# Turning x and x1 by transfers of squares and VectorE's transposes: two attention layers on one core

## The chip, the core and the metric

The kernel runs on one core of a Trainium2 chip. The metric is the device time of one execution in microseconds (us): lower is better. The engines named below are TensorE (PE: matmuls, and PEld: its weight loads), VectorE (DVE), ScalarE (ACT), GpSimd (POOL) and SyncE (SP, which here only issues transfers). All data are 32-bit floats. SBUF is the on-chip memory of 128 partitions; PSUM holds what TensorE writes, in banks of 512 floats a partition.

## What is computed

The input is 8 images of 32 x 32 positions with 256 channels, so 1024 rows of 256 for each image. Two layers follow each other:

```python
# layer 0, four heads
q, k, v = split(x @ W_qkv, per head)
a = softmax(q @ k.T / 16)                   # 1024 x 1024 for each head
x1 = concat(a @ v) @ W_out + b_out + x
# layer 1, one head
f, g, h = x1 @ Wf + bf, x1 @ Wg + bg, x1 @ Wh + bh     # f, g: 32 wide; h: 256 wide
y = gamma * (softmax(g @ f.T) @ h) + x1
```

Both layers need their input in two forms. As rows (positions on partitions) x is the value operand of layer 0 and x1 the residual of layer 1. As columns (channels on partitions: x^T and x1^T) they are operands of the score and projection matmuls. The change is about how the second form is made from the first.

## The kernel before

`W_q W_k^T` and `W_v W_out` are folded into one matrix for each head at the start, so that a head needs one projection of x^T. Large matmuls of layer 0 are done by a seven-product scheme on 2 x 2 blocks (`seven`, tasks one, two, three), whose operand sums VectorE makes: `key_sums` from x^T, `value_sums` from x, `sums` from the exponentials, `qsums` from the queries. VectorE also adds the products together when it empties PSUM banks (L252). Within one group of seven products TensorE goes on adding into banks y and z after VectorE has read them, so TensorE's second and third task wait for VectorE's reads of the first and second.

The work is a list of steps. A step is one block of 512 queries of one head of layer 0, or of layer 1. Images follow each other, and the layer-1 unit of image b-1 is put after head 1 of image b (after head 3 for the last image). In step i TensorE computes the scores of step i, and beside them the products of the steps before (`one` is step i-1, `two` is step i-2).

The order in which TensorE, VectorE and ScalarE execute is written out by hand. In the loop over steps (L805) each task gets a place, a number between about 0 and 10, by `put(tasks, places)`; at the end of a step the tasks are sorted by place and emitted. Every engine executes its own instructions in that order, and an instruction that waits holds up all behind it on its engine. Scores stand at 0, 2, 4, 6, 8, 10, the output projection (`project`, L586 and L597) at 3 and 7, the two parts of the products at 5 and 9.

`transpose_rows` (L331 to L344) makes the columns. Each of its four tasks takes a bank of the `psm` pool (2 banks), has TensorE transpose four 128 x 128 blocks of rows into it (L339), and has ScalarE copy the bank into x^T or x1^T (L342). It runs at the start for image 0; in the first block of head 3 for x of the next image, at places 1.5 to 4.5, with `key_sums` at 5.4 to 7.4; in the first block of the head ahead of the layer-1 unit for x1 of the image before, at places 2.5 to 8.5; and at the end for x1 of the last image.

The sums of exponentials go another way: GpSimd adds them over the partitions, and SyncE sends the row through DRAM and back as columns (`line`, L546, then `st`, L549), with `invert` (L555) reading them one step later. These transfers, the loads of x (L120) and the stores of the result (L675, L677) share SyncE's queue.

Buffers that matter: pool `q` has 2 buffers of 128 x 2 x 1024, which hold the queries of a head, or f and g of layer 1; `xT` has 2; `rows` 4; `ps` is 6 PSUM banks for scores and products, `psm` 2.

Of the kernel before, what the change touches and what calls it, by code (L numbers as in the profile page):

```python
# [16 lines left out]
P = 128  # L17
# [3 lines left out]
def kernel(  # L21
# [51 lines left out]
    nc = tc.nc  # L73
    B, H, W, C = x.shape
    N = H * W
    HEADS = w_qkv.shape[1] // (3 * C)
    CK = w_f.shape[1]
    CC = C // P
    NT = N // P
    NB = 512  # L80
    NBLK = N // NB
    HT = NB // P
    HB = NB // 2
    HN = N // 2
# [24 lines left out]
    def tile_of(tag, shape, name):  # L109
        return pools[tag].tile(shape, F32, tag=tag, name=name)  # L110


    rows, rows1 = {}, {}
# [78 lines left out]
    def sum_a(sums, a11, a12, a21, a22):  # L192
        tt = nc.vector.tensor_tensor
        s1, s2, s3, s4 = sums
        return [
            partial(tt, s1, a21, a22, ALU.add),
            partial(tt, s2, s1, a11, ALU.subtract),
            partial(tt, s3, a11, a21, ALU.subtract),
            partial(tt, s4, a12, s2, ALU.subtract),
        ]  # L200
# [128 lines left out]
    xT_of, x1T_of, xblocks, vblocks = {}, {}, {}, {}  # L329

    def transpose_rows(b, src, dst, layer):  # L331


        def task(k, c):
            if b not in dst:
                dst[b] = tile_of("xT", [P, CC, N], f"x{layer}T_{b}")
            pt = tile_of("psm", [P, NB], f"px{layer}_{b}_{k}_{c}")
            for t in range(HT):
                nc.tensor.transpose(  # L339
                    pt[:, ts(t, P)], src[b][:, k * HT + t, ts(c, P)], ident  # L340
                )
            nc.scalar.copy(dst[b][:, c, ts(k, NB)], pt)  # L342

        return [partial(task, k, c) for k in range(NBLK) for c in range(CC)]  # L344

    def key_sums(b):

        made = {}

        def piece(i):  # L350
            if i == 0:
                xT = xT_of[b]
                t = tile_of("v", [P, 4, HN], f"xs_{b}")
                sums = [t[:, k, :] for k in range(4)]
                blocks = [xT[:, c, ts(k, HN)] for k in range(2) for c in range(CC)]
                made["l"] = sum_a(sums, *blocks)
                xblocks[b] = a_operands(blocks, sums)
            made["l"][i]()

        return [partial(piece, i) for i in range(4)]  # L360
# [75 lines left out]
    class Layer0:  # L436
        def __init__(self, b, h):
            self.b, self.h, self.name = b, h, f"{b}_{h}"
            self.p, self.y, self.r = {}, {}, {}
            self.products_of, self.pblocks = {}, {}  # L440
            self.first = (b * HEADS + h) * NBLK * HT

        def queries(self):

            b, h = self.b, self.h

            def quarter(d, k):
                if d == 0 and k == 0:
                    self.q = tile_of("q", [P, CC, N], f"q_{self.name}")
                return self.q[:, d, ts(k, HN)].unsqueeze(1)  # L450

            def after():
                t = tile_of("qs", [P, 3, NBLK, HB], f"qs_{self.name}")
                q = self.q.rearrange("p c (k e i) -> p c e k i", k=NBLK, e=2)
                blocks = [q[:, c, e] for c in range(CC) for e in range(2)]
                sums = [blocks[1]] + [t[:, k] for k in range(3)]
                self.pieces = sum_b(sums, *blocks)
                self.blocks = b_operands(blocks, sums)

            def piece(k):  # L460
                self.pieces[k]()  # L461

            return seven(
                f"q_{self.name}", NB, 1,
                lambda number: [(0, wblocks[h][number], xblocks[b][number])],
                {
                    "11": lambda: quarter(0, 0), "12": lambda: quarter(1, 0),
                    "21": lambda: quarter(0, 1), "22": lambda: quarter(1, 1),
                },
                WIDE, nc.scalar.copy, after,  # L470
            ), [partial(piece, k) for k in range(4)]
# [132 lines left out]
    class Layer1:  # L604
        scale = 1.0

        def __init__(self, b):
            self.b, self.name = b, f"{b}_l1"
            self.s = {}

        def store_fg(self, d, k, pm):

# [5 lines left out]
        def queries(self):  # L618
            b = self.b

            def start():
                t = tile_of("q", [P, 2, N], f"fg_{b}")
                self.f, self.g = t[:, 0, :], t[:, 1, :]

            return [start] + project_T(
                f"fg_{b}", lambda: wfg_sb, P, lambda: x1T_of[b], self.store_fg
            )
# [122 lines left out]
    def weave(*lists):  # L750
# [12 lines left out]
        s=2, rows=4, xT=2, v=2, q=2, qs=2, xt=1, ss=1, s2=1, s3=1, m0=1, rs=1, rb=1,  # L763
# [32 lines left out]
    def is_l0(s):  # L796
        return s is not None and isinstance(s[0], Layer0)

    def step(k):
        return steps[k] if 0 <= k < len(steps) else None  # L800
# [4 lines left out]
    for i, (a, blk) in enumerate(steps):  # L805
        l0 = isinstance(a, Layer0)
        one, two, nxt = step(i - 1), step(i - 2), step(i + 1)
        places = []

        def put(tasks, *at):  # L810
            assert len(tasks) == len(at)
            places.extend(zip(at, range(len(places), len(places) + len(at)), tasks))

        if l0:
            put(a.scores(blk), 0, 2, 4, 6, 8, 10)
        else:
            tasks, pieces = a.scores(blk)
            put(tasks, *((0.5, 2.4) if blk == 0 else (0.5, 2)))
            put(pieces, *((1.6, 3.9, 6.2, 6.5, 7.4, 8.4, 8.6) if blk == 0 else
                          (0.9, 2.7, 4.2, 5, 6.2, 6.8, 7.5)))  # L820
        if is_l0(two):
            u, k = two
            put(u.products_of[k][2:], 1 if l0 else 0)
            put([partial(u.invert, k)], 2.9 if l0 or blk == 1 else 1.9)
            put(u.project(k), *((3, 7) if l0 else (2, 6) if blk == 0 else (3, 7)))
        if is_l0(one):
            u, k = one
            sums, keys = u.sums(k)
            u.products_of[k] = u.products(k)
            put(sums[:2] + sums[3:], *((2.2, 3.2, 4.2) if l0 else (0.8, 2.2, 4.5)))  # L830
            put(sums[2:3], 5.2 if l0 else 5.5)
            put(keys, *((6.2, 8.2) if l0 else (7.6, 9.6)))
            put(u.products_of[k][:2], *((5, 9) if l0 else (4, 7)))
        elif one is not None:
            put(one[0].products(one[1]), *((3, 5, 7, 9) if l0 else (1, 4, 6, 8)))
        if i == 0:
            fold = fold_weights(1) + fold_weights(2) + fold_weights(3)
            put(fold, -2, -1, *[0.9 + 0.6 * n for n in range(len(fold) - 2)])
        if i == 1:
            put([partial(nc.vector.tensor_scalar, bh_sb, bh_sb, gamma_sb, None, ALU.mult)], 8.5)  # L840

        if is_l0(nxt) and blk == NBLK - 1:
            queries, qsums = nxt[0].queries()
            put(queries, *((2.5, 4.5, 6.5) if not l0 else
                            (1.5, 2.5, 4.5) if is_l0(two) else (0.5, 2.5, 5.5)))
            put(qsums, *((6.7, 6.9, 7.3, 7.6) if not l0 else
                          (5.4, 6.4, 7.2, 7.4) if is_l0(two) else (6.4, 7.2, 7.3, 7.4)))

        if l0 and a.h == 0 and blk == 0:
            put(residual(a.b), 5.3, 6.3, 7.3, 7.4)  # L850
        if l0 and a.h == 0 and blk == 1:
            put(value_sums(a.b), 1.4, 2.4, 3.4, 4.4)
        if l0 and a.h == 2 and blk == 0 and a.b + 1 < B:
            load_x(a.b + 1)
        if l0 and a.h == HEADS - 1 and blk == 0 and a.b + 1 < B:
            put(transpose_rows(a.b + 1, rows, xT_of, 0), 1.5, 2.5, 3.5, 4.5)
            put(key_sums(a.b + 1), 5.4, 6.4, 7.2, 7.4)

        if l0 and a.b > 0 and a.h == behind(a.b) - 1:
            if blk == 0:  # L860
                put(transpose_rows(a.b - 1, rows1, x1T_of, 1), 2.5, 4.5, 6.5, 8.5)
            else:
                put(nxt[0].queries(), 1.4, 1.5, 3.5)
        if not l0 and blk == 0:
            put(a.values(), 0.9, 1, 3, 5, 8)
        if nxt is None:
            put(transpose_rows(B - 1, rows1, x1T_of, 1), 8.1, 8.2, 8.3, 8.4)
            put(final.queries(), 9, 9.1, 9.3)
        for _, _, t in sorted(places, key=lambda x: x[:2]):
            t()  # L870
# [82 lines left out]
    with tc.If(bad > 0), ExitStack() as general:  # L953
        open_pools(general, "g", dict(
            s=2, rows=2, xT=2, v=2, q=2, m0=1, y=1, rs=1, rb=2, r=8, ps=6, psm=2,
# [3 lines left out]
        for b in range(B):  # L959
# [3 lines left out]
            for h in range(HEADS):  # L963
                a = General0(b, h)
# [4 lines left out]
            a = Layer1(b)  # L969
# [37 lines left out]
```

## Time and profile before

The time is 2381.99 us, the median of 3 runs (2380.85 to 2382.96). The profiled execution spans 2379.7 us.

| engine | busy us | share of the span |
|---|---|---|
| TensorE, matmuls | 2361.3 | 99% |
| TensorE, weight loads | 1948.2 | 82% |
| VectorE | 1585.2 | 67% |
| ScalarE | 621.9 | 26% |
| GpSimd | 236.4 | 10% |
| transfers, main queue | | 3.2% of 16 engines |

Busy time counts how long an engine had an instruction in it; matmuls overlap each other, so a busy TensorE can hold short pauses, and the duration of one matmul is longer than the distance from its start to the next. A row of a group gives line, engine, operation, out<-in, shapes and count; after the bar the busy time and the mean of one in ns; after the second bar how long the engine stood idle just before these instructions, and what ended most of that idleness. A row of the timeline gives start (us from the span's beginning), duration, engine, line, operation, and the number of instructions merged into it.

### The profile page before, as it was taken

The numbers are of one execution on the slowest core, as the hardware profiler recorded it, in microseconds if no ns is written. First come the engines' busy times: TensorE is split into PE (matmuls) and PEld (weight loads), VectorE is DVE, ScalarE is ACT, GpSimd is POOL, SyncE is SP. The second block draws the span as 40 slices with busy tenths as digits, with TensorE's granted clock in tenths as the row PEclk, the third lists the DMA queues.
The fourth block names the chain that finished last, engine by engine and source line by source line (L and its number), as shares of the span: only waits on it lengthen the run. The fifth ranks groups of instructions, "written<-read, shape, count | busy, mean of one in ns | idle before, by whom it ended". The sixth has DMA issues, their size and how long they took to land.

```text
span 2379.7 us, 25958 instructions
## 1 busy us (share of the span) xinstructions
PE 2361.3 (99%) x10608; PEld 1948.2 (82%) x10608; DVE 1585.2 (67%) x2477; ACT 621.9 (26%) x1001; POOL 236.4 (10%) x93
## 2 busy tenths in 40 slices
PE   8999999999999999999999999999999999999999
PEld 6888888788887888788887888878888788888877
DVE  5667767567675666766667567676676756766665
ACT  2222223222232222322123222232222322122232
POOL 0111100011110111101111011110011101001110
PEclk9999999999999999999999999999999999999999
DMA  3000000000000000000000000000000000000000
GB/s 118 1 1 1 1 18 1 18 1 4 16 1 18 1 19 1 1 18 1 18 1 1 18 1 18 1 1 18 1 18 1 1 19 1 1 1 1 1 10 29
DMA packets 43535, 23.63 MB, mean 10 GB/s; under 512 B 36048, under 2 KB 38096, under 8 KB 43408
## 3 DMA queue, kind: packets, MB, share of 16 engines
q1 hardware_dynamic: 43408, 21.90, 3.2%
q8 instruction: 85, 1.39, 0.2%
q14 instruction: 42, 0.34, 0.1%
HBM read 13.37 MB, written 8.52 MB: 9 GB/s over the span
## 4 chain that ended last, share of the span: by engine, by line
PE 96%; DVE 3%; DMA 0%; issue 0%; ACT 0%; SPq 0%; DVEq 0%; ACTq 0%
PE psy L235 14%; PE psy_y L235 14%; PE pa_l L730 9%; PE po L586 9%; PE psx L235 9%; PE psz L235 9%; PE psx_y L235 9%; PE psz_y L235 9%; PE psy_q L235 3%; PE psx_q L235 2%; PE psz_q L235 2%; PE pr_v_l L419 2%; PE pm_fg L399 1%; PE ps_l L651 1%; PE px L339 1%; DVE s_l L712 1%
## 5 line engine op out<-in xcount | busy, mean ns | idle before, releaser
L542 POOL PARTITION_ALL_REDUCE rb<-rs x64 | 206.9, 3233 | 1914.8 <-DVE rs L540 1914.8
L490 ACT ACTIVATE p<-p 128x1024 f32<-128x1024 f32 x128 | 135.3, 1057 | 494.4 <-DVE p L252 494.4
L235 PE MATMUL psy<-qs,xs 128*128 128x256 f32 x1024 | 262.9, 379 | 1.3 <-DVE qs L461 1.3
L235 PE MATMUL psx<-q,x0T 128*128 128x256 f32 x1024 | 262.8, 379 | 0.0
L235 PE MATMUL psz<-q,xs 128*128 128x256 f32 x1024 | 262.8, 379 | 0.0
L235 PE MATMUL psy_y<-s,xt 128*128 128x256 f32 x1024 | 242.5, 380 | 1.5 <-DVE xt L374 1.2
L586 PE MATMUL po<-wvo,y 128*128 128x256 f32 x1024 | 242.1, 379 | 0.0
L235 PE MATMUL psx_y<-p,x 128*128 128x256 f32 x1024 | 242.0, 379 | 0.0
L730 PE MATMUL pa_l<-v_l,s_l 128*128 128x257 f32 x1024 | 231.7, 381 | 2.3 <-DVE y L252 1.9
L235 PEld LDWEIGHTS psx<-q,x0T 128*128 128x128 f32 x1024 | 193.9, 190 | 42.6 <-issue 18.6
L730 PEld LDWEIGHTS pa_l<-v_l,s_l 128*128 128x128 f32 x1024 | 193.8, 190 | 39.0 <-issue 12.7
L586 PEld LDWEIGHTS po<-wvo,y 128*128 128x128 f32 x1024 | 192.9, 190 | 38.8 <-issue 15.1
L235 PEld LDWEIGHTS psx_y<-p,x 128*128 128x128 f32 x1024 | 193.0, 190 | 33.0 <-issue 8.6
L235 PEld LDWEIGHTS psy_y<-s,xt 128*128 128x128 f32 x1024 | 193.2, 190 | 31.1 <-issue 4.0
L235 PEld LDWEIGHTS psy<-qs,xs 128*128 128x128 f32 x1024 | 194.6, 190 | 28.0 <-DVE qs L461 1.7
L235 PEld LDWEIGHTS psz<-q,xs 128*128 128x128 f32 x1024 | 194.7, 190 | 26.3
L252 DVE TENSOR_TENSOR u<-psy,e 128x512 f32<-128x512 f32 x128 | 88.5, 691 | 156.9 <-PE psy L235 83.8
L264 ACT ACTIVATE p<-psx 128x512 f32<-128x512 f32 x128 | 76.4, 597 | 378.5 <-PE psx L235 378.4
L252 DVE TENSOR_TENSOR v<-psy,e 128x512 f32<-128x512 f32 x128 | 88.2, 689 | 113.1 <-PE psy L235 112.9
L235 PE MATMUL psy<-qs,x0T 128*128 128x256 f32 x512 | 131.4, 379 | 0.0
L597 DVE SCALAR_TENSOR_TENSOR x<-po,inverse,x 128x256 f32<-128x256 f32 x256 | 112.0, 479 | 25.7 <-PE po L586 15.6
L258 ACT COPY e<-psx 128x512 f32<-128x512 f32 x128 | 73.8, 576 | 209.7 <-PE psx L235 209.7
(108 smaller groups left out, 3151.7 us busy)
## 6 DMA issues: line engine op xcount, KB each, us to landing
out_dram<-x SPq DMA_DIRECT2D x15, 512.0 KB, 2.6
x<-in_x_dram SPq DMA_DIRECT2D x14, 512.0 KB, 4.4
w<-in_L_conv_W_qkv_dram SPq DMA_DIRECT2D x4, 768.0 KB
x<-in_x_dram SPq DMA_DIRECT2D x4, 256.0 KB, 4.7
w<-in_L_conv_W_out_dram SPq DMA_DIRECT2D x4, 256.0 KB, 9.7
line<-rb SPq DMA_DIRECT2D x64, 2.0 KB
st<-line SPq DMA_DIRECT2D x64, 2.0 KB, 2.1
out_dram<-x SPq DMA_DIRECT2D x4, 128.0 KB, 2.1
```

The source lines that it names most:

```text
L235: nc.tensor.matmul(banks[k][:, ts(i, w)], lhsT=lhsT, rhs=rhs, start=first and n == 0, stop=True, skip_group_check=True,)
L252: nc.vector.tensor_tensor(dst, shaped(banks[k]), shaped(other), ALU.add)
L258: nc.scalar.copy(scratch("e"), banks["x"])
L264: copy(outs["11"](), shaped(banks["x"]))
L339: nc.tensor.transpose(pt[:, ts(t, P)], src[b][:, k * HT + t, ts(c, P)], ident)
L399: nc.tensor.matmul(pm[:m], lhsT=w()[:, c, d * P : d * P + m], rhs=src()[:, c, ts(k, NB)], start=(c == 0), stop=(c == CC - 1),)
L419: nc.tensor.matmul(pm[:, ts(j, C)], lhsT=src()[:, c, ts(2 * t2 + j, P)], rhs=w()[:, c, :], start=(c == 0), stop=(c == CC - 1),)
L490: exp(both, both)
L542: nc.gpsimd.partition_all_reduce(t, r.rearrange("p e i -> p (e i)"), P, bass_isa.ReduceOp.add)
L586: nc.tensor.matmul(pm[:, ts(j, C)], lhsT=self.y[blk][:, c, ts(2 * t2 + j, P)], rhs=folded[self.h][1][:, c, :], start=(c == 0), stop=(c == ...
L597: nc.vector.scalar_tensor_tensor(acc, pm[:, ts(j, C)], inverse[:, n : n + 1], acc, ALU.mult, ALU.add)
L730: nc.tensor.matmul(pm[:, : C + 1], lhsT=p[:, j, ts(ti, P)], rhs=v[:, j, : C + 1], start=(j == 0), stop=(j == NT - 1),)
```

## The change

For x of images 1 to 7 and x1 of images 0 to 6, TensorE and ScalarE no longer make the columns. `turn_rows` does it in two stages. First `move`: transfers within SBUF carry 32 x 32 squares to the place on the partitions where they belong after the turn, still unturned, into a scratch buffer. There are 4 calls of `move` with 4 transfers each; one transfer takes 32 partitions to 32 others, 16 squares side by side, so 16 pieces of 128 bytes for each partition. Then `piece`: VectorE transposes each square, 128 x 512 at a time, from the scratch into x^T or x1^T, in 4 instructions.

The scratch is the `q` buffer that the unit two steps later is going to use for its queries (or for f and g): `q_tile` and `fg_tile` take that buffer early. The moves stand at places 0.1 to 0.4 of the step, the pieces at 3.4 to 5.6 (x) or 5.4 to 7.4 (x1), and the key sums move from 5.4, 6.4, 7.2, 7.4 to 6.4, 6.6, 7.2, 7.4. What it is for: to take the transposes out of TensorE's instruction stream.

```diff
+    def turn_rows(b, src, dst, layer, scratch):
+        Q = 32
+        def move(a):
+            to, rows_v = (
+                t.rearrange("p u n -> p (u n)").rearrange("p (s q) -> p s q", q=P)
+                for t in (scratch(), src[b])
+            )
+            for q in range(P // Q):
+                nc.sync.dma_start(to[ts(q, Q), :, ts(a, Q)], rows_v[ts(a, Q), :, ts(q, Q)])
+        def piece(k, c):
+            if b not in dst:
+                dst[b] = tile_of("xT", [P, CC, N], f"x{layer}T_{b}")
+            squares = scratch()[:, k, :].rearrange("p (t c q) -> p t c q", c=CC, q=P)
+            nc.vector.transpose(
+                dst[b][:, c, ts(k, NB)].rearrange("p (t q) -> p t q", q=P), squares[:, :, c, :]
+            )
+        return (
+            [partial(move, a) for a in range(P // Q)],
+            [partial(piece, k, c) for k in range(NBLK) for c in range(CC)],
+        )
...
+        def q_tile(self):
+            if self.q is None:
+                self.q = tile_of("q", [P, CC, N], f"q_{self.name}")
+            return self.q
...
         if l0 and a.h == HEADS - 1 and blk == 0 and a.b + 1 < B:
-            put(transpose_rows(a.b + 1, rows, xT_of, 0), 1.5, 2.5, 3.5, 4.5)
-            put(key_sums(a.b + 1), 5.4, 6.4, 7.2, 7.4)
+            moves, pieces = turn_rows(a.b + 1, rows, xT_of, 0, step(i + 2)[0].q_tile)
+            put(moves, 0.1, 0.2, 0.3, 0.4)
+            put(pieces, 3.4, 4.4, 5.4, 5.6)
+            put(key_sums(a.b + 1), 6.4, 6.6, 7.2, 7.4)
...
             if blk == 0:
-                put(transpose_rows(a.b - 1, rows1, x1T_of, 1), 2.5, 4.5, 6.5, 8.5)
+                moves, pieces = turn_rows(a.b - 1, rows1, x1T_of, 1, step(i + 2)[0].fg_tile)
+                put(moves, 0.1, 0.2, 0.3, 0.4)
+                put(pieces, 5.4, 6.4, 7.2, 7.4)
```

Layer 1 gets an `fg_tile` of the same kind as `q_tile`.

More of the change, by code (lines that the diff above doesn't have):

```diff
@@ L441, in __init__ @@
             self.first = (b * HEADS + h) * NBLK * HT
+            self.q = None
+        def q_tile(self):
+            if self.q is None:
+                self.q = tile_of("q", [P, CC, N], f"q_{self.name}")
+            return self.q
         def queries(self):
@@ L447, in quarter @@
             def quarter(d, k):
-                if d == 0 and k == 0:
-                    self.q = tile_of("q", [P, CC, N], f"q_{self.name}")
-                return self.q[:, d, ts(k, HN)].unsqueeze(1)
+                return self.q_tile()[:, d, ts(k, HN)].unsqueeze(1)
             def after():
@@ L609, in __init__, with fg_tile @@
             self.s = {}
+            self.fg = None
+        def fg_tile(self):
+            if self.fg is None:
+                self.fg = tile_of("q", [P, 2, N], f"fg_{self.b}")
+            return self.fg
         def store_fg(self, d, k, pm):
@@ L621, in start @@
             def start():
-                t = tile_of("q", [P, 2, N], f"fg_{b}")
+                t = self.fg_tile()
                 self.f, self.g = t[:, 0, :], t[:, 1, :]
```

## The prediction, made before the change was run

> **What bounds the kernel now.** I read the page's busy shares first, then the chain that ended last, then the groups of the operations the diff touches, then the timeline of one step that the change rewrites, and last the queue that will carry the new transfers.
>
> ```profile
> span 2379.7 us, 25958 instructions
> PE 2361.3 (99%) x10608; PEld 1948.2 (82%) x10608; DVE 1585.2 (67%) x2477; ACT 621.9 (26%) x1001; POOL 236.4 (10%) x93
> PE 96%; DVE 3%; DMA 0%; issue 0%; ACT 0%; SPq 0%; DVEq 0%; ACTq 0%
> ```
>
> TensorE is busy 99% of the span and carries 96% of the chain; the waits before its rows are a few us in all. So TensorE's instruction stream is the time, and an instruction taken out of it shortens the kernel, unless a wait takes its place.
>
> ```profile
> L339 PE MATMUL px<-ident,x 128*128 128x128 f32 x256 | 40.0, 283 | 5.7 <-DMA x<-in_x_dram 5.4 <-ACT x1T L342 0.2
> L342 ACT COPY x0T<-px 128x512 f32<-128x512 f32 x32 | 18.6, 581 | 49.0 <-PE px L339 49.0
> L342 ACT COPY x1T<-px 128x512 f32<-128x512 f32 x32 | 18.4, 582 | 21.3 <-PE px L339 21.3
> L137 DVE STREAM_TRANSPOSE row<-col 128x32 f32<-128x32 f32 x1 | 0.2, 211 | 0.0
> ```
>
> These are the transposes (groups, shapes kept apart). The 283 ns is a pipelined matmul's length, not its price. The price is read from starts in the timeline of the first step in which x is turned for the next image (head 3 of image 0, first block, 203.69 to 233.07):
>
> ```profile
> 209.73 0.60 PE L339 MATMUL px<-ident,x 128*128 128x128 f32 x4
> 210.17 1.03 PE L235 MATMUL psx<-q,x0T 128*128 128x256 f32 x4
> ...
> 212.34 1.89 PE L586 MATMUL po<-wvo,y 128*128 128x256 f32 x8
> 214.06 0.60 PE L339 MATMUL px<-ident,x 128*128 128x128 f32 x4
> 214.50 1.03 PE L235 MATMUL psy<-qs,x0T 128*128 128x256 f32 x4
> ```
>
> Four transposes hold TensorE 0.44 us (209.73 to 210.17, 214.06 to 214.50). The same stretch on VectorE and SyncE:
>
> ```profile
> 214.57 0.17 DVE L555 RECIPROCAL inverse<-st 128x4 f32<-128x4 f32 x1
> 214.84 0.88 DVE L597 SCALAR_TENSOR_TENSOR x<-po,inverse,x 128x256 f32<-128x256 f32 x2
> 215.63 1.22 DVE L529 TENSOR_TENSOR s<-ss,p 128x1024 f32<-128x1024 f32 x1
> 216.76 0.69 DVE L252 TENSOR_TENSOR p<-psy,e 128x512 f32<-128x512 f32 x1
> ```
> ```profile
> 206.17 0.36 SPq L549 DMA_DIRECT2D st<-line  x1
> 234.25 0.23 SPq L546 DMA_DIRECT2D line<-rb  x1
> ```
>
> In that step, and in the one that turns x1 (327.97 to 357.35), the table of windows gives TensorE 100% and VectorE 19.66 and 17.35 of 29.38 us. SyncE is free from 206.53, 2.84 us into the step, until the step is over.
>
> **What the Trainium skill says.** "VectorE: DVE Perf Modes", section "The three transpose paths": VectorE turns 32x32 blocks only, and goes SBUF to SBUF. Hence the squares must first be carried to their place by transfers; this trace has only one 128x32 case (211 ns). "Vector Engine (DVE) Microarchitecture Reference", section 3.8: the transpose sustains one element per cycle per lane. At the 0.96 GHz of the first page's specifications 512 elements are an estimated 0.53 us plus a fixed part; no 512-wide transpose is in this trace. "DMA: Bandwidth & Descriptors", specifications: pieces under 512 B are below line rate; its section "Why small descriptors are slow (HBM only)" says that transfers within SBUF escape most of that. The trace has 128-byte pieces only from HBM and no transfer within SBUF, so it can't confirm the second.
>
> **The change, part by part.**
>
> *Removed.* x of images 1 to 7 and x1 of images 0 to 6: 14 turns of 4 tasks, 56 tasks. On TensorE 56 x 0.44 = 24.4 us, all on the path (1.0% of the time; the chain puts px at 1%). On ScalarE 56 copies x 0.58 = 32 us, which lay beside TensorE's work: worth nothing. Image 0's x and image 7's x1 keep their old way.
>
> *VectorE's pieces.* 56 transposes of 128x512. Low end 0.53 us (the skill's rate), high end 0.9 (0.17 for the shortest operations here, plus (211-167)/32 = 1.4 ns an element from the 128x32 row). I take 0.65, as for other f32 operations of this size: 2.6 us more in a step with 9.7 or 12.0 us free. That is hidden, but it is added where VectorE has no gaps: 212 to 219 and from 223 on it runs almost without pause, in the x step with key_sums behind.
>
> *The transfers.* A turn is 16 transfers, each 32 partitions x 16 pieces of 128 B: 512 pieces, 64 KB; 8192 pieces and 1.05 MB in all. They wait for the end of the last step's scores (the q buffer they use as scratch is then free) and for SyncE (2.84 us into the step). Issue: st, with as many pieces, takes 0.36 us; with the gap to the next about 0.41, so 6.6 us for 16. Landing of a lone one: 2.1 us for st. Pace of the pieces: the last wfg_sb transfer is 256 pieces of 128 B, and in the window of 20.0 to 20.5 us the slices in its middle run at 82 to 113 GB/s. At 100 GB/s a turn takes 10.5 us. So:
> - low: issue sets the pace, 2.84 + 6.6 + 2.1 = 11.5 us into the step;
> - middle: 2.84 + 1 until the first piece + 10.5 + 0.4 = 14.7;
> - high: transfers don't overlap. st's burst takes 0.9 us of its 2.1: 16 x 0.9 = 14.4, so 2.84 + 1 + 14.4 + 0.2 = 18.4.
>
> *The new wait.* The first piece reads parts of all 16 transfers, so VectorE stands until the last has landed, and what is queued behind it stands too. For x it stands at place 3.4, behind s<-ss,p, whose end is at 216.76; with the two tasks removed ahead of it (0.87), that is 12.2 us into the step. Behind it are the adds that empty the scores' banks (places 4, 6, 8), on which TensorE waits when it writes those banks again. I followed VectorE's queue with the durations above. In the changed step TensorE comes to the third part of the scores, place 10, at 25.9 us into the step (231.35 - 203.69, less four tasks), and v<-psy,e of place 8 must have read its bank by then. VectorE's work from place 3.4 to that add, by the distance of its starts in the timeline, is 12.0 us (two sums and m 3.4, 4 pieces 2.6, 4 key sums 2.4, the adds p, p, u, v 2.4, x<-po 0.8, u_y 0.4). Starting at 12.2 it ends at 24.2: 1.7 us to spare. Hence a landing up to 13.9 us costs TensorE nothing, and each us later costs about one. For x1 the pieces stand at 5.4, which VectorE reaches at 345.3 - 327.97 - 0.87 = 16.5, with no key sums behind: landings up to about 19 are free.
>
> *The rest.* Keys moved from 5.4 to 6.4: nothing before the next step needs them, hidden. q and fg taken a step earlier: their buffer is free from the last step's scores. st of the step before is ahead of the transfers on the queue, the next line is at 234.25, after them: no delay for inverse.
>
> *Sum.* Landing at 14.7: 7 x 0.8 = 5.6 us lost of 24.4. Landing at 11.5: nothing lost. I take 3.5, as issue and pace may overlap better than the short burst shows: 24.4 - 3.5 = 20.9, and 2382.0 - 20.9 = 2361.
>
> **The rivals.**
> - *Late landing eats it (B).* At 16 us each x step loses 2.1, 15 in all: 2372; at 17 it loses 3.1, 22 in all: 2379. For it: no trace shows back-to-back transfers of 512 pieces. Against: within SBUF, by the skill, small pieces go better than from HBM.
> - *The transfer becomes the bound (C).* At 18.4 the x steps lose 4.5 each, 31 us, x1 none: 2382 - 24.4 + 31 = 2389; if a transfer took twice st's burst (landing near 33) the x steps would lose 19 each and the x1 steps 14 each: 231 us, 2589. For it: VectorE's wait in order stops TensorE. Against: the pace of 100 GB/s seen.
> - *VectorE becomes the bound in the x step without any late landing (D).* If a transpose takes 0.9 us, 4 x 0.25 = 1 us more, still inside 1.7. With 1.2 us it is 2.2 more, 0.5 lost in each of 7 steps: 2361. The free 9.7 us a step speak against more.
> - *Nothing gained.* If the transposes had lain in a wait of TensorE: 2382. The starts above are back to back, so I give it no more than 2 in 100.
>
> **How the numbers follow.** Forecast case (landing up to 15, 2355 to 2365): 0.63. B: 0.18, of which 0.06 lies within 0.2% (2377.2 to 2386.8). C: 0.15. D: 0.02; nothing gained: 0.02. Faster: 0.63 + 0.12 + 0.02 = 0.77; same: 0.06 + 0.02 = 0.08; slower: 0.15. The lower end of the range is the full 24.4 and an allowance of 2.6 us for short waits around the removed tasks: 2355. The upper end takes in B whole and the mildest of C: 2384.
>
> **What would show it.** In the profile after: px 32 instead of 256, copies 4 and 4; 56 STREAM_TRANSPOSE of 128x512 near 0.65 us; 224 transfers of 64 KB; both steps at 27.6 us rather than 29.4. In the x step the idle time before the first transpose, with the transfer as its releaser, gives the landing: under 2 us, I am right; 4 to 5 us, B; more, and psy or psz waiting for DVE in the list of waits, C. Wrong altogether if the x1 steps also wait, or if TensorE's steps don't shrink though no transpose waits.

## The result, and the profile after

The changed kernel takes 2374.05 us (median of 6 runs, 2372.63 to 2376.01), beside 2381.1 us for the kernel before on the same chip: a ratio of 0.9971, 95% interval 0.9958 to 0.9984. So it is faster by 7 us, a third of the forecast 20.9. The top of the page after:

```profile
span 2373.4 us, 25982 instructions
PE 2342.1 (99%) x10384; PEld 1923.1 (81%) x10384; DVE 1616.1 (68%) x2533; ACT 589.8 (25%) x945; POOL 236.4 (10%) x93
PE 86%; DVE 8%; SPq 3%; issue 1%; DMA 1%; POOL 1%; ACT 0%; DVEq 0%; POOLq 0%; ACTq 0%
```

The third line is the chain that ended last, by engine. TensorE lost the 224 transposes, and its share of the chain went from 96% to 86%: VectorE and, new, SyncE's issuing of transfers now lie on the path. The groups show where (line 364 is `piece`; the last bar gives the idle time ahead of it and its releaser):

```profile
L364 DVE STREAM_TRANSPOSE x0T<-q 128x512 f32<-128x512 f32 x28 | 18.9, 696 | 27.1 <-DMA q<-x 27.1
L364 DVE STREAM_TRANSPOSE x1T<-fg 128x512 f32<-128x512 f32 x28 | 18.9, 695 | 0.0
L339 PE MATMUL px<-ident,x 128*128 128x128 f32 x32 | 6.3, 356 | 4.4 <-DMA x<-in_x_dram 4.2 <-ACT x1T L342 0.2
```

VectorE stood 27.1 us in all ahead of the pieces of x, for the transfers, and not at all ahead of those of x1. The step of image 3, which turns x for image 4, shows what the wait did. First SyncE, which issues the transfers (timeline), then VectorE, then TensorE:

```profile
1078.85 0.24 SPq L577 DMA_DIRECT2D line<-rb  x1
1079.19 1.27 SPq L358 DMA_DIRECT2D q<-x  x2
1080.55 0.57 SPq L580 DMA_DIRECT2D st<-line  x1
1081.17 9.35 SPq L358 DMA_DIRECT2D q<-x  x14
```
```profile
1087.45 1.22 DVE L560 TENSOR_TENSOR s<-ss,p 128x1024 f32<-128x1024 f32 x1
1092.31 0.71 DVE L364 STREAM_TRANSPOSE x0T<-q 128x512 f32<-128x512 f32 x1 [3.64 <-DMA q<-x]
1092.94 0.65 DVE L252 TENSOR_TENSOR p<-psy,e 128x512 f32<-128x512 f32 x1
...
1098.52 0.65 DVE L252 TENSOR_TENSOR u<-psy,e 128x512 f32<-128x512 f32 x1
...
1103.53 0.69 DVE L252 TENSOR_TENSOR v<-psy,e 128x512 f32<-128x512 f32 x1
```
```profile
1092.35 1.03 PE L235 MATMUL psx<-q,x0T 128*128 128x256 f32 x4
1093.65 1.13 PE L235 MATMUL psy<-qs,xs 128*128 128x256 f32 x4 [0.27 <-DVE p L252]
...
1097.21 1.03 PE L235 MATMUL psx<-q,x0T 128*128 128x256 f32 x4
1099.22 1.13 PE L235 MATMUL psy<-qs,xs 128*128 128x256 f32 x4 [0.99 <-DVE u L252]
...
1101.92 1.89 PE L235 MATMUL psy_y<-s,xt 128*128 128x256 f32 x8
1104.27 1.13 PE L235 MATMUL psy<-qs,x0T 128*128 128x256 f32 x4 [0.46 <-DVE v L252]
```

The step begins at 1075.95. Its 16 transfers occupy SyncE without a gap from 1079.19 to 1090.52, the first transpose starts at 1092.31 (16.36 us into the step), and TensorE then stands three times, each time at the y bank of a group of scores, for the add that VectorE has not made yet: p at place 6, u at place 8, v at place 10. By the starts, 1.30 where 0.86 is the rule, 2.01 where 0.86, and 2.35 where 1.73: 2.2 us, and with the 0.1 us that the first matmuls after each wait need more, 2.5.

For each of the seven x steps I took the start of the first transpose from the step's start as the landing, and the step's length less 27.63 us (the length where nothing waits) as the loss. All numbers are us, the first two counted from the step's start:

| x for image | first transfer issued | landing | TensorE's loss |
|---|---|---|---|
| 1 | 1.64 | 15.08 | 1.25 |
| 2 | 3.24 | 16.35 | 2.52 |
| 3 | 3.24 | 16.93 | 3.10 |
| 4 | 3.24 | 16.36 | 2.52 |
| 5 | 3.24 | 16.52 | 2.69 |
| 6 | 3.23 | 17.10 | 3.26 |
| 7 | 3.23 | 17.86 | 4.02 |

In every row the loss is the landing less 13.83 us. The losses add up to 19.4 us, more than the 12.3 that the x steps gain. The x1 steps lost nothing.

### The profile page after: what moved, and what is told of

It reads as the page before. It is cut to its first block, busy times and chain, and to the rows that moved or that the text cites. A ratio compares the mean times of both kernels' runs of the same rounds, so it can differ in the third digit from the quotient of the medians.

```text
span 2373.4 us, 25982 instructions
## 1 busy us (share of the span) xinstructions
PE 2342.1 (99%) x10384; PEld 1923.1 (81%) x10384; DVE 1616.1 (68%) x2533; ACT 589.8 (25%) x945; POOL 236.4 (10%) x93
## 4 chain that ended last, share of the span: by engine, by line
PE 86%; DVE 8%; SPq 3%; issue 1%; DMA 1%; POOL 1%; ACT 0%; DVEq 0%; POOLq 0%; ACTq 0%
PE psy L235 12%; PE psy_y L235 12%; PE pa_l L767 9%; PE po L617 8%; PE psx L235 8%; PE psz L235 8%; PE psx_y L235 8%; PE psz_y L235 8%; PE psy_q L235 3%; SPq L358 3%; PE psx_q L235 2%; PE psz_q L235 2%; PE pr_v_l L446 2%; PE pm_fg L426 1%; PE ps_l L688 1%; DVE m L565 1%
## 5 line engine op out<-in xcount | busy, mean ns | idle before, releaser
L617 PEld LDWEIGHTS po<-wvo,y 128*128 128x128 f32 x1024 | 194.5, 190 | 40.0 <-issue 15.1
L767 PEld LDWEIGHTS pa_l<-v_l,s_l 128*128 128x128 f32 x1024 | 193.7, 190 | 39.0 <-issue 12.7
L235 PE MATMUL psz_y<-ss,x 128*128 128x256 f32 x512 | 120.9, 379 | 0.0
```

The source lines that it names most:

```text
L235: nc.tensor.matmul(banks[k][:, ts(i, w)], lhsT=lhsT, rhs=rhs, start=first and n == 0, stop=True, skip_group_check=True,)
L617: nc.tensor.matmul(pm[:, ts(j, C)], lhsT=self.y[blk][:, c, ts(2 * t2 + j, P)], rhs=folded[self.h][1][:, c, :], start=(c == 0), stop=(c == ...
L767: nc.tensor.matmul(pm[:, : C + 1], lhsT=p[:, j, ts(ti, P)], rhs=v[:, j, : C + 1], start=(j == 0), stop=(j == NT - 1),)
```

## The experiments

Ratios are to the kernel before, on the same chip in the same runs, with 95% intervals.

**Each half alone.** x1 only puts the old way of x back:

```diff
-            moves, pieces = turn_rows(a.b + 1, rows, xT_of, 0, step(i + 2)[0].q_tile)
-            put(moves, 0.1, 0.2, 0.3, 0.4)
-            put(pieces, 3.4, 4.4, 5.4, 5.6)
-            put(key_sums(a.b + 1), 6.4, 6.6, 7.2, 7.4)
+            put(transpose_rows(a.b + 1, rows, xT_of, 0), 1.5, 2.5, 3.5, 4.5)
+            put(key_sums(a.b + 1), 5.4, 6.4, 7.2, 7.4)
```

> x of later images is turned by TensorE again (old places), only x1 by transfers. Late-landing theory: the x1 steps gain 7 x 1.75 = 12.3 us and lose nothing, so 2369 to 2370, faster than the changed kernel by about 5. Rival (both halves share the loss, for example because VectorE is busier everywhere): half of the changed kernel's gain of 7, so 2377 to 2378.

Measured: 2370.36 us, 0.9953 (0.9937 to 0.9970). x only puts the old way of x1 back in the same manner.

> x1 is turned by TensorE again (old places), only x by transfers. Late-landing theory: the x steps gain 12.3 us by the missing transposes and lose about 17 by VectorE's wait, so 2385 to 2387, slower than before. Rival (shared loss): 2377 to 2378. In each x step VectorE waits 2.4 to 5.1 us ahead of the first piece in either theory.

Measured: 2389.24 us, 1.0029 (1.0020 to 1.0039). The halves have opposite signs: x1 gains 11 us, x loses 7.5 (forecast of the theory: 12 and 3 to 5; it took 17 us for the loss in the x steps, and in this run's trace they lose 19.6). The loss isn't shared.

**The pieces of x later.**

```diff
-            put(pieces, 3.4, 4.4, 5.4, 5.6)
+            put(pieces, 5.4, 5.5, 5.6, 5.7)
```

> As the changed kernel, with the four pieces of x at places 5.4 to 5.7 and not 3.4 to 5.6; the key sums and VectorE's amount of work stay. Late-landing theory: the first piece is reached at about 16.4 us into the step and the transfers land at 15 to 18, so the wait falls to under 1.5 us and most of the lost 17 us come back: 2358 to 2363. Rival (VectorE's 2.8 us of added work in a full stretch is what costs): the same work stands later and closer to the key sums, so no gain, 2373 to 2377.

Measured: 2355.56 us, 0.9892 (0.9875 to 0.9908). One line of places brings back 18.5 us, and the time is 2 us below the theory's range. The timeline of image 3's step shows VectorE arriving when the data have landed:

```profile
1082.92 0.43 DVE L252 TENSOR_TENSOR u_y<-psy_y,e_y 128x256 f32<-128x256 f32 x1 [0.17 <-ACT e_y L258]
1083.26 1.22 DVE L560 TENSOR_TENSOR s<-p 128x1024 f32<-128x1024 f32 x1
1084.39 2.48 DVE L364 STREAM_TRANSPOSE x0T<-q 128x512 f32<-128x512 f32 x4
1086.80 0.65 DVE L252 TENSOR_TENSOR u<-psy,e 128x512 f32<-128x512 f32 x1
```

The transfers are issued as before (first one 3.23 us into the step); the four transposes run back to back, about 0.6 us apart, and the work of VectorE is the same. So it was the wait, not the added work. Five of the seven x steps lose nothing now, the other two 0.4 and 0.2 us, with waits of at most 1.2.

**What sets the landing: the pieces, the bytes or the issues?** Half of the squares:

```diff
-                nc.sync.dma_start(to[ts(q, Q), :, ts(a, Q)], rows_v[ts(a, Q), :, ts(q, Q)])
+                nc.sync.dma_start(to[ts(q, Q), ::2, ts(a, Q)], rows_v[ts(a, Q), ::2, ts(q, Q)])
...
-                dst[b][:, c, ts(k, NB)].rearrange("p (t q) -> p t q", q=P), squares[:, :, c, :]
+                dst[b][:, c, ts(k, NB)].rearrange("p (t q) -> p t q", q=P), squares[:, :, 0, :]
```

> Leaves out half of the squares: each of the 16 transfers carries 8 pieces of 128 bytes for each partition and not 16 (32 KB), and the pieces of the second half of the channels read the first half's squares. VectorE's instructions, their places and their order stay. Late-landing theory: if issue time goes with the number of pieces, an issue falls from 0.63 to about 0.35 us, the last landing to about 10 us into the step, no wait, and the whole 24 us show: 2357 to 2359. If issue time is fixed for a transfer, landing and time stay, 2373 to 2375. Rival (VectorE's added work costs): 2373 to 2375 although no transpose waits.

Measured: 2371.29 us, 0.9955 (0.9938 to 0.9971). With half of the pieces and half of the bytes the landing comes only 0.3 to 0.9 us earlier. The view of the issuing line, first in the changed kernel, then here (duration in ns, min/median/max):

```profile
L358 SPq DMA_DIRECT2D q<-x x112: 585/628/1988, 204.4 to 1964.7; - x112
```
```profile
L358 SPq DMA_DIRECT2D q<-x x112: 585/609/763, 205.5 to 1962.1; - x112
```

An issue costs 0.61 us where it cost 0.63, and the time from an issue to its landing fell from 2.3 to 2.0 us in the median; together that is the 0.6 us. The time is just below the range for an issue with a fixed price, as the landing is a little earlier. The losses of this run lie on the same line: landings 14.46 to 17.00, losses 0.62 to 3.16, each the landing less 13.84.

Then the same bytes between the same partitions, in one run of 2 KB for each partition:

```diff
-            to, rows_v = (
-                t.rearrange("p u n -> p (u n)").rearrange("p (s q) -> p s q", q=P)
-                for t in (scratch(), src[b])
-            )
+            to, rows_v = (t.rearrange("p u n -> p (u n)") for t in (scratch(), src[b]))
             for q in range(P // Q):
-                nc.sync.dma_start(to[ts(q, Q), :, ts(a, Q)], rows_v[ts(a, Q), :, ts(q, Q)])
+                nc.sync.dma_start(to[ts(q, Q), ts(a, NB)], rows_v[ts(a, Q), ts(q, NB)])
```

> As the changed kernel, but each of the 16 transfers carries the same 64 KB between the same partitions as one run of 2 KB for each partition, not 16 of 128 bytes: 32 pieces and not 512. The values no longer stand where the squares belong. If the price is per transfer, issue stays near 0.6 us, and time at 2371 to 2375. If the price comes with the three-dimensional pattern or with the count of pieces, issue falls to the 0.36 to 0.46 us of the other transfers, the landing to about 11 us, the wait goes, and the time is 2357 to 2360.

Measured: 2354.78 us, 0.9885 (0.9868 to 0.9901). The expectation on the issue held for the first case and the one on the time for the second, because I had overlooked what this edit does to the wait. The issues and VectorE, image 3:

```profile
1073.31 1.78 SPq L355 DMA_DIRECT2D q<-x  x3
1075.14 0.58 SPq L577 DMA_DIRECT2D st<-line  x1
1075.77 8.15 SPq L355 DMA_DIRECT2D q<-x  x13
```
```profile
1081.59 1.22 DVE L557 TENSOR_TENSOR s<-ss,p 128x1024 f32<-128x1024 f32 x1
1082.72 0.70 DVE L361 STREAM_TRANSPOSE x0T<-q 128x512 f32<-128x512 f32 x1
```

SyncE issues until 1083.92, and the first transpose starts at 1082.72, ahead of the last issue: in this layout a transfer fills one quarter of the columns, so the first two pieces need only 8 of the 16 transfers. An issue still costs 0.59 us (median 588 ns) with 32 pieces in place of 512. So nearly all of the price is per transfer; the pieces matter by 0.04 us. The time is explained by the smaller wait, not by a cheaper issue.

Last, two issuing queues, with every place as in the changed kernel:

```diff
-                nc.sync.dma_start(to[ts(q, Q), :, ts(a, Q)], rows_v[ts(a, Q), :, ts(q, Q)])
+                on = nc.sync if q % 2 == 0 else nc.scalar
+                on.dma_start(to[ts(q, Q), :, ts(a, Q)], rows_v[ts(a, Q), :, ts(q, Q)])
```

> As the changed kernel, all places kept, but every second transfer is issued from ScalarE's queue. Issue theory (a transfer costs its issuing queue about 0.7 us, whatever it carries, and the 16 issues set the landing): two queues at once take 8 x 0.7 = 5.7 us, the last lands 9.5 to 11 us into the step, VectorE (there at 12.7) doesn't wait, 2357 to 2361, the upper end if ScalarE's 5.7 us of issuing hold up the copies that VectorE's adds need. Rival (the transfers themselves, on engines shared by both queues, set the landing): landing stays at 15 to 18 us, 2372 to 2377.

Measured: 2356.01 us, 0.9891 (0.9875 to 0.9908). The issues of the x steps on each queue, and the first pieces' wait:

```profile
L359 ACTq DMA_DIRECT2D q<-x x56: 592/642/919, 204.3 to 1945.4; - x56
L359 SPq DMA_DIRECT2D q<-x x56: 585/624/1072, 204.7 to 1944.3; - x56
```
```profile
L365 DVE STREAM_TRANSPOSE x0T<-q 128x512 f32<-128x512 f32 x28 | 18.9, 694 | 2.0 <-issue 0.9 <-DMA q<-x 0.9
```

An issue still costs 0.62 to 0.64 us on each queue, but eight stand on each; the first transpose starts 12.6 to 13.7 us into the step, under 13.83, and no x step loses anything. The bytes, pieces and places are the same. One rival is left: a queue could also work through its transfers slowly, so that two queues help for that reason. The changed kernel's trace speaks against it. Where it tells the landings of a row of 16 on one queue, the fourth comes 2.3 us after its issue began and the last 2.3 as well (medians over the x steps), so as a rule none waited for those before it. The view of line 358 in the changed kernel:

```profile
DMA to landing us min/median/max: 2.0/2.3/4.1
```

So the issues set the landing. With two queues it was not as early as the 9.5 to 11 expected: ScalarE's own work stands between its issues (in image 3's step its eight took 8.7 us), and the later transfers of a row took longer to land, the last 3.1 us in the median, not 2.3.

**How much of a wait is free.** The pieces of x1 as early as those of x were, with x turned the old way:

```diff
...
-                put(pieces, 5.4, 6.4, 7.2, 7.4)
+                put(pieces, 3.4, 4.4, 5.4, 5.6)
```

> x turned by TensorE as before, x1 by transfers with its pieces as early as those of x (3.4 to 5.6, not 5.4 to 7.4). VectorE will then wait about 3 us ahead of the first piece in each of 7 steps. Slack theory: in the x steps a landing up to 13.8 us was free; here no key sums (2.4 us) stand behind the pieces, so up to 16.2 is free, the transfers land at about 15, and the waits cost TensorE nothing: 2369 to 2372, as with x1 alone. Rival (each us that VectorE waits is lost): 7 x 3 = 21 us more, about 2391.

Measured: 2376.53 us, 0.9979 (0.9971 to 0.9986). VectorE waits 2.1 to 3.9 us ahead of the first piece, 19.9 in all, and the time is 6 us above x1 alone. Neither expectation held: about two thirds of the waits are free, not all and not none. Then the changed kernel with only the key sums put off to the next step:

```diff
+    later = {}
...
-            put(key_sums(a.b + 1), 6.4, 6.6, 7.2, 7.4)
+            later[i + 1] = key_sums(a.b + 1)
+        if i in later:
+            put(later[i], 0.5, 0.6, 0.7, 0.8)
```

> The changed kernel with its early pieces of x, and only the four key sums put off to the next step (places 0.5 to 0.8). VectorE's waits ahead of the first piece stay at 2.4 to 5.1 us. Slack theory: 2.4 us less work behind the pieces, so landings up to 16.2 us are free, and of the landings at 15.1 to 17.9 only the excess costs, 3 to 5 us in all in place of 19: 2358 to 2362. Rival (each us that VectorE waits is lost, or TensorE stands at the banks ahead of the key sums): 2371 to 2375.

Measured: 2370.56 us, 0.9956 (0.9939 to 0.9972): 3.5 us below the changed kernel, where I had expected some 14. The rival had expected no gain, but it named what happened: TensorE standing at banks whose adds come ahead of the key sums. TensorE's timeline, image 3:

```profile
1090.82 1.03 PE L235 MATMUL psx<-q,x0T 128*128 128x256 f32 x4
1092.11 1.13 PE L235 MATMUL psy<-qs,xs 128*128 128x256 f32 x4 [0.27 <-DVE p L252]
...
1097.69 1.13 PE L235 MATMUL psy<-qs,xs 128*128 128x256 f32 x4 [0.99 <-DVE u L252]
...
1100.38 1.89 PE L235 MATMUL psy_y<-s,xt 128*128 128x256 f32 x8
1102.11 1.03 PE L235 MATMUL psy<-qs,x0T 128*128 128x256 f32 x4
```

The third wait (for v, behind the key sums) is gone; the first two, whose adds stand ahead of the key sums, are as long as they were. In all seven steps the loss is now the landing less 14.57, and the losses add up to 13.9 us in place of 19.4. So there are several deadlines, one each time TensorE writes a y bank again. The add of v, for place 10, allowed a landing at 13.83; the add of u, for place 8, allows 14.57; the add of p, for place 6, about 15.9 (16.36 less the 0.44 us lost there). The key sums stand between the adds of u and v, so putting them off moves only v's deadline. The x1 steps with early pieces, which have no key sums, show the same limit: in each of the seven the loss is the landing (14.77 to 16.65) less 14.57, 7.0 us in all.

**Both remedies at once.** Late pieces and the last two key sums put off to places 0.6 and 0.7 of the next step:

```diff
+    later = {}
...
-            put(pieces, 3.4, 4.4, 5.4, 5.6)
-            put(key_sums(a.b + 1), 6.4, 6.6, 7.2, 7.4)
+            put(pieces, 5.4, 5.5, 5.6, 5.7)
+            keys = key_sums(a.b + 1)
+            put(keys[:2], 7.2, 7.4)
+            later[i + 1] = keys[2:]
+        if i in later:
+            put(later[i], 0.6, 0.7)
```

> Pieces of x at 5.4 to 5.7 and the last two key sums put off to places 0.6 and 0.7 of the next step, where VectorE has gaps. Theory: late pieces alone left waits of up to 1.2 us ahead of the first piece in the last images; 1.2 us less work behind them takes up what these cost, at most 2 us in all: 2354 to 2356. Rival (the remaining waits cost nothing): the same as late pieces alone, 2355 to 2356.

Measured: 2356.22 us, 0.9892 (0.9876 to 0.9909), the same as late pieces alone: in the trace no x step loses anything now, but the 0.6 us that were left are too small for the times to show. Nothing is left to gain there: late pieces, two queues and this one agree within their intervals, at 26 us below the kernel before, and late pieces are the smallest edit.

## Why the prediction was right or wrong

*What is removed: right.* Each removed task shortened TensorE's order by 0.44 us, in 56 places. With the wait out of the way the whole gain of 24.4 us appears: late pieces are 26.1 us below the kernel before. The 1.7 us more are within the spread between runs of one kernel (2378.8 to 2383.1 for the kernel before).

*VectorE's pieces: right.* A 128x512 transpose takes 0.70 us, and in a row the next starts after about 0.6; I had 0.65. The Trainium skill's page "Vector Engine (DVE) Microarchitecture Reference", section 3.8, led to an estimated 0.53 and a fixed part, which agrees. The added 2.8 us in a step cost nothing by themselves: with late pieces they are all there.

*The new wait, its place and its price: right.* VectorE arrived at place 3.4 12.7 us into the step (12.2 forecast: I took off both tasks removed by then, 0.87 us, but the add of v at 212.10, with which VectorE's run of work begins, has only the one at 209.73 ahead of it, 0.44). A landing up to 13.9 us was to be free and each us after it to cost one. Measured: 13.83, and one for one. The single deadline that I worked out, place 10, happened to be the first to be missed; that another follows 0.7 us behind it I did not see, and it misled two of my expectations.

*x1: right.* No wait, no loss; 11 us gained alone.

*The landing: wrong, and this is the step that failed.* The forecast had 14.7 as the middle and then took a loss of only 3.5 us, as if transfers landed at 14.4 ("issue and pace may overlap better than the short burst shows"). They landed at 15.1 to 17.9, 16.6 in the mean. As seven steps lose one us for each us of delay, these 2.2 us are 15 us of time; that is the gain of 20.9 that was forecast less the 7 that came, within the spread between runs. The term was made of these parts:
- The start, the largest: 1.3 us in six of the seven steps, about 8 us of time. I read SyncE's free moment (2.84 us into the step, after `st`) in one step, that of image 0, where `line` goes out at 1.3. There the transfers landed at 15.08, 0.4 from the middle value. In the six others `line` goes out at 2.9 and `st` has been issued at 5.2, with two of the transfers ahead of it; the landing is 16.35 at the earliest. By the written places, the step before has there a layer-1 unit two steps back, its query sums stand later, and so do the sum that GpSimd waits for (it ends 0.5 us ahead of the step in the trace before, and 2.1 us ahead in image 0), GpSimd's sum and `line`. The view was in the trace before: `line` at 498.87 in the step that starts at 495.97. No run moved `line` alone; this is read from the comparison of the steps.
- The issue, with the wrong limit. I priced a transfer at st's 0.36 us and 0.05 to the next, 6.6 us for 16, and took the pieces' pace (10.5 us at 100 GB/s) for the slower of the two. An issue within SBUF costs 0.63, and 16 of them with st in between take 11.3 us. So the issues were the limit; that the pace gave nearly the same length was luck, and the miss from it in the step that I had read is only 0.4 us. The pace I worried about was no limit here: with two queues 16 transfers went out in 8 to 9 us, and halving the pieces brought 0.3 to 0.9 us.
- The 0.3 us by which I went under my own middle value, for an overlap that no trace had shown; about 2 us of time.
- Single transfers that took longer: in the steps for images 3, 6 and 7 the landing is 0.6 to 1.5 us later than in those for images 2 and 4, about 3 us of time. For images 6 and 7 the last issue took 1.37 and 1.99 us. Why stays open.

*The rivals.* B, the late landing, is what happened: it gave 2372 for a landing at 16 and 2379 at 17, and 2374 at 16.6 was measured. I named its price right and gave it too small a chance, because the middle value was built from one burst and one step. The signs fit it only in part: VectorE's wait ahead of the first piece was 2.4 to 5.1 us, 3.9 in the mean, where 4 to 5 was to tell B, and TensorE stood at psy for VectorE, which I had listed for C alone.

*What the Trainium skill says of issuing.* "Perfetto Trace Analysis", section "What "DMA-bound" means", names the issuing sequencer as a possible limit, seen as a solid track of slices; here SyncE's track is solid for 11.3 us, which agrees. It says that large descriptors help then: 2 KB pieces in place of 128 bytes took 0.59 in place of 0.63 us, so on this limit they hardly do. "DMA: Bandwidth & Descriptors", section "Issuing engines are not separate DMA queues", says that issuing from several engines saves only issue time, usually small; here the second queue took VectorE's wait ahead of the pieces of x from 27.1 to 2.0 us, 18 us of the kernel's time.

## What to carry to other kernels

When a change adds a row of transfers that one reader waits for, price the issues first: count the transfers on a queue, multiply by the issue of a like one (both ends within SBUF if that is what they are), and compare with the moment at which the first reader needs the last one. A wait of an engine that isn't the bound is free up to the first deadline of the one that is; list all deadlines behind the wait, since a remedy that relaxes only one moves the loss to the next. And read the start of such a chain in several steps, not in the first that comes to hand.

## What the runs showed of the hardware

- Issuing a transfer within SBUF from SyncE takes 0.63 us with 512 pieces, 0.61 with 256 and 0.59 with 32, and the next follows after about 0.04 more. A single `st` between DRAM and SBUF takes 0.36; in the 14 steps with such transfers, between them, the same `st` takes 0.43 to 0.57. Why an issue in such a row is dearer was not tried, and stays open.
- 64 KB within SBUF in 512 pieces of 128 bytes land 2.3 us after their issue began (median), about as a lone 2 KB `st` (2.1); with pieces of 2 KB it is 2.0.
- ScalarE's queue issues at the same price as SyncE's (0.64 us), and the two overlap. With both in use the time from issue to landing grows along a row, from 2.1 to 2.3 us at first to 3.1 for the last of an x step; on one queue it stays at 2.3.
- VectorE's waits aren't lost time one for one: with x1's pieces early, 19.9 us of them cost 6 us.
